# Layer 1's value products in 64x64 quadrants, with the second part moved behind the next half step's first scores

## The chip, the cores and the metric

The kernel runs on one core of a Trainium2 chip. A core has a matrix engine (TensorE, PE in the profile, with its weight loads shown apart as PEld), a vector engine (VectorE, DVE), a scalar engine (ScalarE, ACT), GpSimd (POOL) and a sync engine (SyncE, SP), which here issues nearly all DMA transfers. The metric is the device time of one execution in microseconds (us). Three runs of the kernel before took 4215.25 to 4218.63 us, with a median of 4215.89.

## What is computed

The input is a batch of 8 images with 512 channels of 32 x 32 pixels, so 1024 tokens each, in fp32. Two attention layers follow one another, each with a residual connection and a group normalization ahead of it. Layer 0 is ordinary attention with 8 heads of 64 channels. Layer 1, where the change lies, mixes the heads' scores before its softmax and normalizes the result over a whole head:

```python
attn = jnp.einsum('bhdq,bhdT->bhqT', q, k) * scale
attn = jnp.einsum('gh,bhqT->bgqT', w_head, attn)
attn = jax.nn.softmax(attn, axis=-1)
mean = jnp.mean(attn, axis=(-2, -1), keepdims=True)
var = jnp.var(attn, axis=(-2, -1), keepdims=True)
attn = (attn - mean) / jnp.sqrt(var + EPS)
attn = attn * in_gamma[None, :, None, None] + in_beta[None, :, None, None]
out = jnp.einsum('bhqT,bhdT->bhqd', attn, v)
```

After that come a projection with a bias and the residual.

## The kernel before

Layer 0 runs for all images first, layer 1 after it, image by image. The order of the instructions on every engine is the order in which the program writes them: nothing is rearranged by a scheduler[...]. An agenda (`ag`) holds pieces of work for fixed half steps.

In layer 1 an image has 4 blocks of 256 queries, and each block meets 4 blocks of 256 keys. Each of these 16 raw tiles is worked on in two half steps, so there are NX = 32 half steps `x`, and a few more in which the last ones drain. `half_step` interleaves three stages of different age:

- `scores(x, i)`, for i = 0 and 1: two heads each time, 8 matmuls in 64x64 quadrants, into one of three rotating PSUM tiles "m" of two banks. ACT or DVE copies the tile to `raw`. DVE does it for i = 0 in odd half steps, ACT for the rest. From half step 5 on, each part of the scores lets SP issue one piece of the next image's data or weights.
- `regroup`: eight DMA transfers of 256 KB (`re<-raw`) bring one raw tile into the order in which heads can be mixed, one region r each. One is issued after each part of a mix and each part of the value products, held by `behind` until the last matmul of that part is done.
- `mix(y, j)`, with y = x - 4: 32 matmuls of 64x64 with the head weights, region by region in the order `R_ORDER`, so the last 8 of its 64 records in the trace need the region that was sent last. ACT takes the exponential into `e` (two tiles rotate).
- With w = x - 5: `squares` on ACT, `sum_e` and `sum_e2` on DVE, and `values(w, 0)` and `values(w, 1)` on PE. Each part of the value products covers four heads, two in each column half, with all 128 keys as the contracted dimension; it adds to one of two accumulators `acc` of one PSUM bank each.

After every eighth value step the accumulators are copied out (`leave`), and `totals` sums the rows with 8 matmuls of 32 columns of weights (L1781). In fp32 a matmul shows as two records in the trace, each with a weight load before it, so 8 matmuls of scores are 16 matmul records, a mix part is 64, a value part is 8.

The instructions of one half step on PE stand in this order: scores part one, mix part one, value part one, scores part two, mix part two, value part two. On ACT: squares, scores copy (even half steps), squares, exponential, scores copy, exponential.

Of the kernel before, what the change touches and what calls it, by code (L numbers as in the profile page):

```python
# [18 lines left out]
P = 128  # L19
# [448 lines left out]
def tile_two_attention_layers(  # L468
# [19 lines left out]
    nc = tc.nc  # L488
    B, C, T = x_d.shape
    H = w_head.shape[0]  # L490
    D = C // H
    NCC = C // P
    NT = T // P
# [5 lines left out]
    Q8 = D // H  # L499
# [71 lines left out]
    NQB = 4  # L571
# [32 lines left out]
    class GroupStats:  # L604
# [3 lines left out]
        def __init__(self, pool, psum, mv, nm, keep=3):  # L608
            self.keep = keep
            self.pool, self.psum, self.mv, self.nm = pool, psum, mv, nm  # L610
            self.w = mv.shape[1]
# [85 lines left out]
    with ExitStack() as l0:  # L697
# [87 lines left out]
        n_t, xa_t, q_t, k_t, v_t = {}, {}, {}, {}, {}  # L785
# [415 lines left out]
        for b in range(B):  # L1201
            more = b + 1 < B
            ag = Agenda()
# [61 lines left out]
    with ExitStack() as l1:  # L1265
# [14 lines left out]
        NX = 2 * NQB * NKB  # L1280
        QLAG = NX // NQB
        R_ORDER = (0, 4, 1, 5, 2, 6, 3, 7)
        MLAG = 4

        def m_psum(nm):
            return ps_m.tile([P, 2, FB], F32, tag="m", name=nm)
# [4 lines left out]
        y_t, qo_t, k_t, v_t = ({0: t["1"]} for t in (n_t, q_t, k_t, v_t))  # L1291
        w_t = {}

        def behind(dma, ins):

            tc.add_manual_dep(
                dma.ins,
                ins.ins.name,
                mybir.DependencyInfo(
                    mybir.DependencyClass.Sync, mybir.DependencyReason.DATA  # L1300
                ),
                reason="one at a time",
            )
# [158 lines left out]
        def k_leave():  # L1462
            for fn in due:
                fn()
            due.clear()
# [173 lines left out]
        class Attention1:  # L1639
            def __init__(self, b):  # L1640
                self.b = b
                self.raw, self.re, self.e, self.e2 = {}, {}, {}, {}
                self.due, self.pieces = [], []

            def scores(self, x, i):

                b, t, hp = self.b, x // 2, x % 2 * 2 + i
                qb, kb = t // NKB, t % NKB
                nm = f"s1_{b}_{x}_{i}"
                ps = m_psum(nm)  # L1650
                pv = ps.rearrange("p m (j k) -> p m j k", j=2)
                for j in range(2):
                    for c in range(2):
                        for m in range(2):
                            r = slice(m * D, m * D + D)
                            last = nc.tensor.matmul(  # L1656
                                pv[c * D : c * D + D, m, j],
                                qo_t[b][r, 2 * qb + j, hp, ts(c, D)],
                                k_t[b][r, hp, ts(kb, KB)], start=True, stop=True,
                            )  # L1660
                if x > MLAG:
                    self.piece(last)
                if x % 2 and i == 1:
                    self.due = [(t, r) for r in R_ORDER]
                if x % 2 == 0 and i == 0:
                    self.raw[t] = rawpool.tile([P, H, 2, KB], F32, tag="raw", name=f"raw_{b}_{t}")
                dst = self.raw[t][:, 2 * hp : 2 * hp + 2]
                if i == (x == 0) and (x < MLAG or x % 2):
                    nc.vector.tensor_copy(dst, pv)  # L1669
                else:  # L1670
                    nc.scalar.copy(dst, pv)  # L1671

            def regroup(self, ins=None, n=1):

# [63 lines left out]
            def values(self, y, w):  # L1738

                b, t, kc = self.b, y // 2, y % 2  # L1740
                kc = t % NKB * 2 + kc
                if kc == 0 and w == 0:
                    self.acc = [
                        ps_a.tile([P, 2, QB], F32, tag=f"a{i}", name=f"a1_{b}_{y}_{i}")
                        for i in range(2)
                    ]
                e = self.by_head(self.e[y].rearrange("p j c -> p (j c)"))
                for g in range(4 * w, 4 * w + 4):
                    s, two = g // 2 % 2, g % 2
                    last = nc.tensor.matmul(  # L1750
                        self.acc[w][two * D : two * D + D, s].rearrange(
                            "p (c i) -> p c i", i=Q8
                        ),
                        v_t[b][:, kc, ts(g, D)], e[:, g],
                        start=(kc == 0 and s == 0), stop=(kc == NT - 1),
                        skip_group_check=True,
                    )
                self.regroup(last)

            def leave(self, qb):  # L1760
# [115 lines left out]

            def half_step(self, x, ag):
                y, w = x - MLAG, x - MLAG - 1
                if 0 <= w < NX:
                    self.squares(w, 0)  # L1880
                    self.sum_e(w, 0)
                if x < NX:
                    self.scores(x, 0)
                if 0 <= w < NX:
                    self.squares(w, 1)
                    self.sum_e(w, 1)
                if x < NX + MLAG:
                    k_leave()
                if 0 <= w < NX:
                    self.sum_e2(w, 0)  # L1890
                    self.sum_e2(w, 1)
                k_leave()
                if 0 <= y < NX:
                    self.mix(y, 0)
                if 0 <= w < NX:
                    self.values(w, 0)
                if x < NX:
                    self.scores(x, 1)
                if 0 <= y < NX:
                    self.mix(y, 1)  # L1900
                if x < MLAG or x >= NX:

                    self.regroup(n=NR if x != MLAG - 1 else 5)
                if x >= NX:
                    self.piece(n=len(self.pieces))
                ag.run(x - 0.5)
                if 0 <= w < NX:
                    self.values(w, 1)
                    self.e.pop(w)
                    if w % QLAG == QLAG - 1:  # L1910
                        qb = w // QLAG
                        self.leave(qb)
                        self.totals(qb)
                        if qb < NQB - 1:
                            ag.at(x + 2, lambda: self.reciprocals(qb, ag, x + 2))
                            ag.at(x + 6, lambda: self.divide(qb))
                ag.run(x)

        def load_wv_again(b):
# [7 lines left out]
        for b in range(B):  # L1927
            more = b + 1 < B
            a = Attention1(b)
            ag = Agenda()  # L1930
# [131 lines left out]
```

## Time and profile before

| What | Value |
|---|---|
| Median of three runs | 4215.89 us |
| Profiled execution, its span | 4215.8 us |
| PE busy | 4147.3 us (98%) |
| DVE busy | 2868.0 us (68%) |
| ACT busy | 2318.4 us (55%) |
| Layer 1's scores (L1656) | 552.0 us, 8192 records |
| Layer 1's mixes (L1704) | 596.5 us, 32768 records |
| Layer 1's value products (L1750) | 556.2 us, 4096 records |
| Granted PE clock | 0.999 |

The profiled execution is as long as the median of the runs. The span is that of the program's own instructions. Busy times of different lines may overlap. A line of the profile gives the source line, the engine, the operation, the tiles written and read, and the number of records. In brackets or after a second bar stands the idle time of the engine before the instruction and what ended it; "issue" means that the profile shows nothing that the engine waited for. A timeline or a chain has the start and the length in microseconds first. A matmul's end in the records is modelled, and records overlap, so a time from one start to the next is the surer measure.

Layer 1's half steps begin at about 1800 us. The second image's scores start at 2115.3 us and the third's at 2425.1.

### The profile page before, as it was taken

Reading aid. Unit: us, or ns where it says so; the run is one execution under the profiler, and the core shown is the slowest. Engines: PE = TensorE matmul, PEld = TensorE weight load, DVE = VectorE, ACT = ScalarE, POOL = GpSimd, SP = SyncE. Lnnn points to the kernel's source line nnn. Section 1 sums busy time; section 2 is a strip of 40 time slices with the busy share of each in tenths; the row PEclk is TensorE's granted clock in tenths of the full one; section 3 lists DMA queues with packets and bytes.
Section 4 is the critical chain, followed back from the end, with each engine's and each line's share of the span. In section 5 each row is a group of like instructions: output and inputs, shape, how many; then the busy total and the mean of one; then the engine's idle time right before and its main releaser. Section 6 shows DMA issues by size and latency. Waiting matters only on the chain.

```text
span 4215.8 us, 131422 instructions
## 1 busy us (share of the span) xinstructions
PE 4147.3 (98%) x58572; PEld 2216.2 (53%) x58572; DVE 2868.0 (68%) x3779; ACT 2318.4 (55%) x2735; POOL 60.3 (1%) x86
## 2 busy tenths in 40 slices
PE   8999999999999999999999999999999999999998
PEld 4353535353535353466466466466466466465565
DVE  5748484848484747568668668578578588587587
ACT  2717171727272625258268278278287287286386
POOL 0000000000000000000000000000000000000000
PEclk9999999999999999999999999999999999999999
DMA  4212121212121212167467377377386386485575
GB/s 132 97 65 94 59 101 50 82 45 84 48 84 48 84 48 84 62 156 196 131 170 188 121 189 189 108 201 190 104 206 177 112 208 159 129 209 145 148 180 138
DMA packets 257905, 529.35 MB, mean 126 GB/s; under 512 B 52336, under 2 KB 59888, under 8 KB 250672
## 3 DMA queue, kind: packets, MB, share of 16 engines
q1 hardware_dynamic: 254752, 520.15, 43.5%
q8 instruction: 461, 7.55, 0.8%
q0 software_dynamic: 2576, 0.69, 0.4%
q14 instruction: 116, 0.95, 0.1%
HBM read 204.50 MB, written 46.92 MB: 60 GB/s over the span
## 4 chain that ended last, share of the span: by engine, by line
PE 93%; DMA 2%; DVE 2%; ACT 1%; issue 1%; SPq 0%; DVEq 0%; ACTq 0%
PE a L1750 12%; PE m L1704 12%; PE s L1656 11%; PE s L1082 10%; PE a L1108 10%; PE pk_p L902 5%; PE pq_p L902 5%; PE pv_p L902 5%; PE pp_p L902 5%; PE pk L1400 4%; PE pq L1400 4%; PE pv L1475 4%; PE pp L1400 3%; PE t L1781 1%; DMA re<-raw 1%
## 5 line engine op out<-in xcount | busy, mean ns | idle before, releaser
L1704 PEld LDWEIGHTS m<-wmix,re 64*64 64x64 f32 x32768 | 583.6, 135 | 119.6 <-issue 53.5
L1087 ACT ACTIVATE e<-s 128x1024 f32<-128x1024 f32 x512 | 497.2, 1026 | 234.3 <-PE s L1082 233.8
L1704 PE MATMUL m<-wmix,re 64*64 64x64 f32 x32768 | 596.5, 219 | 21.1 <-issue 14.0
L1710 ACT ACTIVATE e<-m 128x1024 f32<-128x1024 f32 x512 | 525.2, 1026 | 141.9 <-PE m L1704 137.2
L1728 DVE TENSOR_TENSOR z<-z,e 128x1024 f32<-128x1024 f32 x448 | 538.0, 1219 | 68.8 <-ACT e L1710 68.7
L1732 DVE TENSOR_TENSOR z<-z,e 128x1024 f32<-128x1024 f32 x448 | 535.1, 1220 | 66.3 <-ACT e L1721 64.7
L1750 PE MATMUL a<-e,v 128*64 128x256 f32 x4096 | 556.2, 392 | 1.7 <-issue 1.0
L1656 PE MATMUL s<-k,q 64*64 64x256 f32 x8192 | 552.0, 388 | 5.0 <-DVE q L1512 2.7
L1095 DVE TENSOR_TENSOR zacc<-zacc,e 128x1024 f32<-128x1024 f32 x384 | 468.7, 1221 | 79.1 <-ACT e L1087 56.8
L1671 ACT COPY raw<-s 128x1024 f32<-128x1024 f32 x368 | 372.6, 1013 | 265.5 <-PE s L1656 226.5
L1082 PE MATMUL s<-q,k 64*64 64x512 f32 x4096 | 490.1, 593 | 2.3 <-ACT e L1087 2.3
L1108 PE MATMUL a<-e,v 64*64 64x512 f32 x4096 | 484.0, 589 | 0.0
L1721 ACT ACTIVATE e<-e 128x1024 f32<-128x1024 f32 x448 | 459.8, 1056 | 0.0
L1656 PEld LDWEIGHTS s<-k,q 64*64 64x64 f32 x8192 | 268.5, 132 | 267.8 <-issue 164.4
L1750 PEld LDWEIGHTS a<-e,v 128*64 128x64 f32 x4096 | 250.8, 136 | 122.5 <-issue 14.0
L1108 PEld LDWEIGHTS a<-e,v 64*64 64x64 f32 x4096 | 156.7, 133 | 282.8 <-issue 282.5
L1082 PEld LDWEIGHTS s<-q,k 64*64 64x64 f32 x4096 | 147.9, 133 | 275.2 <-issue 241.0
L1669 DVE COPY raw<-s 128x1024 f32<-128x1024 f32 x144 | 175.9, 1222 | 93.5 <-PE s L1656 89.7
L1093 DVE TENSOR_TENSOR zacc<-e,e 128x1024 f32<-128x1024 f32 x64 | 78.3, 1223 | 53.6 <-ACT e L1087 53.6
L1475 PE MATMUL pv<-wv,y 128*128 128x512 f32 x256 | 114.1, 599 | 0.5 <-DVE raw L1669 0.5
L1480 DVE COPY v<-pv 128x512 f32<-128x512 f32 x30 | 20.7, 690 | 136.0 <-ACT v L1479 136.0
L902 PE MATMUL pv_p<-left_v,tmp 128*128 128x256 f32 x512 | 113.1, 379 | 0.0
(316 smaller groups left out, 4162.7 us busy)
## 6 DMA issues: line engine op xcount, KB each, us to landing
re<-raw SPq DMA_DIRECT2D x1024, 256.0 KB
rzb<-zd SPq DMA_DIRECT2D x256, 128.0 KB
left_q<-left_q SPq DMA_DIRECT2D x17, 1792.0 KB
left_p<-left_p SPq DMA_DIRECT2D x17, 1792.0 KB
left_k<-left_k SPq DMA_DIRECT2D x10, 1792.0 KB
x<-in_x_dram SPq DMA_DIRECT2D x32, 512.0 KB
x<-x SPq DMA_DIRECT2D x64, 256.0 KB
left_v<-left_v SPq DMA_DIRECT2D x8, 1792.0 KB
```

The source lines that it names most:

```text
L902: nc.tensor.matmul(out, st, mv, start=start, stop=(k == 1), skip_group_check=True)
L1082: nc.tensor.matmul(ps[c * D : c * D + D, m], k[r, hp, k0 : k0 + D], q[r, hp, ts(f, FB)], start=True, stop=True,)
L1087: nc.scalar.activation(e[i], ps, AF.Exp, scale=S0 * S0)
L1095: nc.vector.tensor_add(zacc[g], zacc[g], e[i])
L1108: nc.tensor.matmul(acc[g][a][m * D : m * D + D], v[rows, kc, ts(2 * hp + m, D)], e[i][rows, m], start=(kc == 0), stop=(kc == NG - 1),)
L1400: nc.tensor.matmul(self.ps[m][:, i], w[:, left, k * HC + i * P : k * HC + i * P + P], right[:, k], start=(k == 0 and m != 2), stop=(k == 1 ...
L1656: last = nc.tensor.matmul(pv[c * D : c * D + D, m, j], qo_t[b][r, 2 * qb + j, hp, ts(c, D)], k_t[b][r, hp, ts(kb, KB)], start=True, stop=True,
L1704: last = nc.tensor.matmul(ps[c * D : c * D + D, a, ts(r, D)], self.re[t, r][rows, j, k0 : k0 + D], wmix[rows].rearrange("p g i -> p (g i)" ...
L1710: nc.scalar.activation(self.e[y][:, j], ps.rearrange("p a c -> p (a c)"), AF.Exp)
L1728: nc.vector.tensor_add(self.z[:, j], self.z[:, j], self.e[y][:, j])
L1732: nc.vector.tensor_add(self.z2[:, j], self.z2[:, j], self.e2[j])
L1750: last = nc.tensor.matmul(self.acc[w][two * D : two * D + D, s].rearrange("p (c i) -> p c i", i=Q8), v_t[b][:, kc, ts(g, D)], e[:, g], sta ...
```

## The change

The value products of the steps 0 to 26 are cut in quadrants: each matmul contracts 64 keys, and the two row halves work at the same time on different heads and in different accumulators. The second part of a step swaps the accumulators between the row halves, and the next step's first part goes on with that assignment. So a step has twice as many matmuls for its value products, 8 in each part (16 records). The last five steps (QF = 5) keep the old shape.

The second part is no longer issued at the end of its half step but in the next one, behind the first part of its scores, together with all that follows it there: the transfer of `regroup`, and, where a query block ends, `leave` and `totals`. Where the next value step begins a new query block, the second part comes ahead of those scores. The first matmul of each second part also waits until the most recent part two of the scores has been copied out of PSUM.

```diff
+        QF = 5
...
+                self.swap = self.late = None
...
                 if i == (x == 0) and (x < MLAG or x % 2):
-                    nc.vector.tensor_copy(dst, pv)
+                    out = nc.vector.tensor_copy(dst, pv)
                 else:
-                    nc.scalar.copy(dst, pv)
+                    out = nc.scalar.copy(dst, pv)
+                if i:
+                    self.swap = out
...
-                for g in range(4 * w, 4 * w + 4):
-                    s, two = g // 2 % 2, g % 2
-                    last = nc.tensor.matmul(
-                        self.acc[w][two * D : two * D + D, s].rearrange(
-                            "p (c i) -> p c i", i=Q8
-                        ),
-                        v_t[b][:, kc, ts(g, D)], e[:, g],
-                        start=(kc == 0 and s == 0), stop=(kc == NT - 1),
-                        skip_group_check=True,
-                    )
+                final = y >= NX - QF
+                for s in range(2):
+                    for n in range(2 if final else 4):
+                        if final:
+                            two, rows, half = n, slice(0, P), w
+                        else:
+                            two, a = n % 2, n // 2
+                            rows, half = slice(a * D, a * D + D), a ^ w ^ y % 2
+                        g = 4 * half + 2 * s + two
+                        last = nc.tensor.matmul(
+                            self.acc[half][two * D : two * D + D, s].rearrange(
+                                "p (c i) -> p c i", i=Q8
+                            ),
+                            v_t[b][rows, kc, ts(g, D)], e[rows, g],
+                            start=(kc == 0 and w == 0 and s == 0),
+                            stop=(kc == NT - 1 and (final or w == 1)),
+                            skip_group_check=True,
+                        )
+                        if w and self.swap is not None:
+                            behind(last, self.swap)
+                            self.swap = None
                 self.regroup(last)
...
             def half_step(self, x, ag):
                 y, w = x - MLAG, x - MLAG - 1
+
+                def finish():
+                    if self.late is not None:
+                        self.late()
+                        self.late = None
+
+                if w % QLAG == 0:
+                    finish()
                 if 0 <= w < NX:
                     self.squares(w, 0)
                     self.sum_e(w, 0)
                 if x < NX:
                     self.scores(x, 0)
+                finish()
...
                 if 0 <= w < NX:
-                    self.values(w, 1)
-                    self.e.pop(w)
-                    if w % QLAG == QLAG - 1:
-                        qb = w // QLAG
-                        self.leave(qb)
-                        self.totals(qb)
-                        if qb < NQB - 1:
-                            ag.at(x + 2, lambda: self.reciprocals(qb, ag, x + 2))
-                            ag.at(x + 6, lambda: self.divide(qb))
+
+                    def second():
+                        self.values(w, 1)
+                        self.e.pop(w)
+                        if w % QLAG == QLAG - 1:
+                            qb = w // QLAG
+                            self.leave(qb)
+                            self.totals(qb)
+                            if qb < NQB - 1:
+                                ag.at(x + 2, lambda: self.reciprocals(qb, ag, x + 2))
+                                ag.at(x + 6, lambda: self.divide(qb))
+
+                    if x + 1 < NX:
+                        self.late = second
+                    else:
+                        second()
                 ag.run(x)
```

## The prediction

> **What bounds the kernel now.** I read the page's busy shares first, then the chain that ended last, then TensorE's (PE's) timeline in single stretches.
>
> ```profile
> PE 4147.3 (98%) x58572; PEld 2216.2 (53%) x58572; DVE 2868.0 (68%) x3779; ACT 2318.4 (55%) x2735; POOL 60.3 (1%) x86
> q8 instruction: 461, 7.55, 0.8%
> ```
>
> PE carries the span. The last column of the first row matters later: 58572 matmul and 58572 weight-load records are 117144 PE instructions. The second row, of the DMA queues, is the traffic that brings instructions: 461 packets and 7.55 MB, so 16 KB or some 255 instructions a packet.
>
> The chain in order of time, at the third image's start (us, length, what):
>
> ```profile
> 2447.12 1.02 PE s L1656 x16
> 2448.15 0.93 PE m L1704 x64
> 2449.08 0.87 PE s L1656 x16
> 2449.95 0.96 PE m L1704 x64
> 2450.91 0.87 PE s L1656 x16
> 2451.77 0.93 PE m L1704 x64
> 2452.70 1.01 PE a L1750 x8
> 2453.72 1.02 PE s L1656 x16
> 2454.74 0.93 PE m L1704 x64
> 2455.67 1.01 PE a L1750 x8
> ```
>
> Scores (s) and mixes (m) are 64x64, value products (a) 128x64. Scores cost 0.87 behind a mix and 1.02 behind value products; these cost 1.01. A round of scores (four quadrants, 256 columns) and a round of value products (two column halves) start 0.216 us apart, so both have 0.86 of work (four rounds) and the rest, about 0.15 on each side, is the change of shape. An undisturbed half step is 2 x (1.02 + 0.93 + 1.01) = 5.92 us (5.94 from start to start).
>
> The half steps are not all undisturbed. From the start of half step 5 to that of 31 the first seven images take 165.2 us on average; less 3 x 1.87 for the row totals (L1781) that is 159.6 / 26 = 6.14 each. PE's timeline shows two kinds of stop, both inside a mix:
>
> ```profile
> 2200.00 0.99 PE L1704 MATMUL m<-wmix,re 64*64 64x64 f32 x56
> 2202.29 0.34 PE L1704 MATMUL m<-wmix,re 64*64 64x64 f32 x8 [1.30 <-DMA re<-raw]
> ```
>
> ```profile
> 2787.88 1.10 PE L1704 MATMUL m<-wmix,re 64*64 64x64 f32 x63
> 2789.55 0.27 PE L1704 MATMUL m<-wmix,re 64*64 64x64 f32 x1 [0.56 <-issue]
> ```
>
> The first waits for the eighth regrouped part of a raw tile (its last 8 matmuls). The second waits for nothing the profile shows. I counted PE instructions from one such "issue" stop to the next: 1024, 3071, 513, 1791, 1024, 1281, 2303 ..., multiples of 256 within two. They are the ends of fetched blocks. In the trace's packet times, 51 such stops of layer 1 have: the next fetch packet starts 1.50 us after the stop (1.06 to 2.4), ends 2.64 after it, and a block's first instruction runs 1.43 (spread 0.10) after its packet ended. So a block asked for when the one before begins is ready 4.07 us later. A half step holds 2 x (32 + 128 + 16) = 352 instructions, 1.375 blocks: 5.60 us of fetching beside 5.92 of work. It is hidden, but barely: these stops cost some 24 us, the re<-raw ones 8.5, in all of layer 1.
>
> [...]
>
> **The change, part by part.** Layer 0 already has value products in quadrants, row halves on different banks:
>
> ```profile
> 200.71 1.90 PE L1108 MATMUL a<-e,v 64*64 64x512 f32 x16
> 202.54 0.64 PE L1127 MATMUL z<-zacc,ones 128*32 128x256 f32 x8
> ```
>
> 16 records of 512 columns in 1.83 us: four at a time, 0.46 a round, where one 128x128 matmul of 512 columns takes 7.06 / 16 = 0.44 (L1475): next to no loss. So I price a 256-column round at 0.216.
>
> 1. Shape. For value steps 0 to 26 (half steps 5 to 31, 54 groups an image, 432 in all) each group goes from 8 records to 16, in four rounds of 0.216: 0.87. Both drains go. A half step of PE work becomes 2 x (0.87 + 0.93 + 0.87) = 5.34, 0.58 less; over 27 x 8 = 216 half steps that is 125 us, if nothing else takes its place. Groups 27 to 31 keep the old shape.
>
> 2. Instructions. 16 more matmuls and their loads per half step: 384 instead of 352, exactly 1.5 blocks. At 4.07 that is 6.10 us, 0.76 more than the new PE work. The cover that hid the fetch is gone: this takes the place of the drains.
>
> 3. Second part behind the next scores. The same PE instructions in another order; nothing is issued twice. Its re<-raw issue on SP's queue moves behind the next scores' piece transfer, so three issues now follow value part two, mix and value part one, 0.87 to 0.93 apart, where eight backlogged ones land about 1.05 apart (2124 to 2130 us). The eighth then lands some 0.3 later. Its landing takes 4.10 us on average from issue now (tiles 2 to 11, spread 0.61; 3.76 for tiles 12 to 14). At the new full speed the mix needs it 4.2 after issue; at the fetch's pace about 4.8. I allow 0.03 us a half step for it.
>
> 4. The new wait, on ScalarE's (ACT's) copy of the second scores. Queued behind it on PE: the mix and the next value part. That mix waited for the same copy, so only 0.87 us of slack goes. ACT has 11 instructions in two half steps, about 0.93 from start to start when back to back: 10.3 us, against 12.2. The copy is done before PE comes to it unless the eighth part is late by a further 0.6. Priced at nothing; without that cover ACT's chain makes a pair of half steps the landing time plus 6.9 us (0.2 to see the landing, four ACT instructions 3.9, then value part two, mix and value part one 2.7, and 0.1 to issue). DVE: 9 x 1.135 = 10.2 us a pair, also covered.
>
> 5. At steps 8, 16 and 24 the second part goes ahead of the first scores, with the accumulators' copies and row totals, as before.
>
> Sum for one image. Half steps 5 to 26 without the two that hold totals: 20 x (6.14 - 6.12) = 0.4 us. Half steps 27 to 31 without one: fewer transfers beside the fetch, which I estimate 0.2 us quicker, so 1.5 x 3.87 = 5.8 plus 0.05 against 6.1: 4 x 0.25 = 1.0. Three with totals: now 8.0; then 5.34 + 1.87 is more than 416 / 256 x 4.07 = 6.6, so PE sets it, with 0.2 for stops 7.4: 1.8. Together 3.2; times 8, 26 us. The profiled execution took 4215.8 us, as the median of the runs, 4215.89, so no correction: 4215.8 - 26 = 4190 us.
>
> The uncertain size is the 4.07. About 36 blocks an image, 288 in all, are paced by it, so 0.1 us is 29 us. It was measured where stops were rare[...]. From below: the shortest start, packet and delay seen (1.06, 0.88, 1.25) make 3.19, and then PE, ACT and landings pace instead. From above: the mean with one spread of its parts, 4.3. I take the mean.
>
> **Rivals.**
> - Fetch stays hidden, because blocks are asked for earlier than I read. Then ACT's chain behind the eighth landing paces: 4.4 + 6.9 = 11.3 us a pair, 5.65 a half step: 20 x 0.49 + 3 x 0.8 + 4 x 0.6 = 14.6 an image, 4099 us. For it: many blocks now pass in 3.55 us without a stop. Against: PE had run ahead there; after a stop the next packet is never sooner than 1.06.
> - Slower, by the fetch[...]. From 4.19 us a block the kernel is over 0.2% slower; at 4.22, 4233 us. For it: single fetches took up to 5.1, and the DMA share is 0.86 in such a stretch (2484 to 2490 us). Against: the pace, and so the traffic, is no higher than now.
> - Quadrants don't run four wide, as e is read with a stride: rounds of 0.43, a group of 1.73, 432 x (1.73 - 1.16) = 246 more, 4460. It decides from 0.29 a round. Against: now both column halves read that stride at full rate.
> - The drain is not the shape's: nothing is saved, the fetch paces, and half steps stay at 6.1 to 6.2: about 4220. Against: scores behind a mix at 0.87.
>
> **Numbers.** The fetch paces near 4.07: 0.52 (4150 to 4222). Fetch hidden: 0.13. Fetch over 4.19: 0.28. Quadrants narrow: 0.03. Drain stays: 0.04. Of the first, 0.11 lies within 0.2% (8.4 us, about what a measurement can tell from no change) and 0.41 below; of the last, 0.02 same and 0.02 slower. So faster 0.54, same 0.13, slower 0.33. The range for 8 in 10, 4125 to 4258, reaches from blocks at 3.85 to 4.3; the likeliest case's own is given above.
>
> **What would show it.** Right: value groups at 64x64 with 0.87 from start to start, scores behind them 0.87, no drains; "issue" stops at most blocks, some three in two half steps, as often in scores and value products as in mixes; half steps near 6.1; PE's busy share lower, with 58572 + 432 x 8 = 62028 records of each kind. Wrong: half steps of 5.6 with waits on ACT or re<-raw (fetch hidden), half steps over 6.3 (fetch slower), value groups over 1.2 us (quadrants narrow).

## The result

The changed kernel is slower. Its median is 4268.93 us (4266.87 to 4272.9), beside 4217.26 us for the kernel before in the same comparison: a ratio of 1.012, with a 95% interval of 1.0106 to 1.0135. The prediction was 4190 us and faster; the sign was wrong, the time missed by 79 us, and it lies above the predicted range (4125 to 4258).

These are the rows of the page of the changed kernel that answer to the first ones shown of before: engine busy times, the queue that brings instructions, and the groups of mixes and value products (busy, mean ns | idle before and what ended most of it).

```profile
PE 4075.1 (95%) x62028; PEld 2355.5 (55%) x62028; DVE 2870.2 (67%) x3779; ACT 2316.2 (54%) x2735; POOL 60.3 (1%) x86
q8 instruction: 488, 8.00, 0.8%
L1708 PE MATMUL m<-wmix,re 64*64 64x64 f32 x32768 | 656.6, 220 | 124.2 <-issue 105.5
L1761 PE MATMUL a<-e,v 64*64 64x256 f32 (+1 forms) x7552 | 577.9, 380 | 16.3 <-ACT raw L1673 9.9
```

PE is busy for 72 us less (4147.3 before), and idle for 124 us more (192.8 of 4267.9 instead of 68.5 of 4215.8). It has the 62028 records and the instruction queue the additional packets that were expected. The idle time lies mostly ahead of mixes.

PE's timeline at the third image shows the new half step (start, length, what; in brackets the idle time just before and what ended it):

```profile
2519.88 1.13 PE L1708 MATMUL m<-wmix,re 64*64 64x64 f32 x64
2520.81 1.06 PE L1658 MATMUL s<-k,q 64*64 64x256 f32 x16
2521.68 1.06 PE L1761 MATMUL a<-e,v 64*64 64x256 f32 x16
2522.54 0.90 PE L1708 MATMUL m<-wmix,re 64*64 64x64 f32 x48
2523.91 0.35 PE L1708 MATMUL m<-wmix,re 64*64 64x64 f32 x8 [0.47 <-issue]
2525.13 0.34 PE L1708 MATMUL m<-wmix,re 64*64 64x64 f32 x8 [0.88 <-DMA re<-raw]
2525.30 1.05 PE L1761 MATMUL a<-e,v 64*64 64x256 f32 x16
2526.16 1.04 PE L1658 MATMUL s<-k,q 64*64 64x256 f32 x16
2527.03 1.11 PE L1708 MATMUL m<-wmix,re 64*64 64x64 f32 x64
```

From start to start a mix takes 0.93 (2519.88 to 2520.81), scores 0.87 (2520.81 to 2521.68, and behind value products 2526.16 to 2527.03) and value products 0.86 (2521.68 to 2522.54 and 2525.30 to 2526.16). In the records of the value products at 2521.68 four records start within 0.04 us and the next four 0.216 later, where the old shape has two records to such a round (2455.60 before): the row halves do work at the same time. The 0.15 us on each side of the value products, which the prediction puts down to the change of shape and calls drains, is gone. In its place the mix at 2522.54 is stopped twice, 0.47 us by nothing that the profile shows and 0.88 by the last regrouped part. So PE is also held back where the profile shows no semaphore. PE's waits over the whole execution (us in total, times, longest):

```profile
PE m L1708 <- issue: 105.5, 130, 2.1
PE m L1708 <- DMA re<-raw: 16.5, 22, 2.4
PE a L1761 <- ACT raw L1673: 9.9, 22, 1.5
PE a L1761 <- issue: 5.6, 11, 1.1
```

The kernel before has, in the same view:

```profile
PE m L1704 <- issue: 14.0, 28, 1.1
PE m L1704 <- DMA re<-raw: 5.7, 10, 1.3
```

This view counts a stop only where the engine's records leave a gap. Counted from start to start, over what a group takes undisturbed, layer 1's stops are: issue 142 us (176 stops) where before had 24 (50), re<-raw 20 (8.5), ACT's copy 11 (0.6), ACT's exponential 6 (0.2). Nearly all issue stops of layer 1 stand at multiples of 256 instructions from one another, before and after, as the prediction read them. Of those in the view of gaps all 31 distances before and all 148 after are such multiples within one, if PE's semaphore instructions are counted too. Every packet of the instruction queue has 16384 bytes, and there are 124056 / 488 = 254 matmul and load instructions to a packet; a packet takes 1.10 us on average, and the first instruction after a stop runs 1.43 us after a packet ended, in both traces. That PE's instructions are fetched in blocks of 256 is read from these numbers.

For all runs below I use one measure beside the time: the mean time from one image's first scores of layer 1 to the next image's, over seven images. It is 307.8 us before and 314.5 after; 8 x 6.7 = 54 us is the whole difference, so it lies in layer 1.

### The profile page after: what moved, and what is told of

It reads as the page before. It is cut to its first block, busy times and chain, and to the rows that moved or that the text cites. A ratio compares the mean times of both kernels' runs of the same rounds, so it can differ in the third digit from the quotient of the medians.

```text
span 4267.9 us, 138296 instructions
## 1 busy us (share of the span) xinstructions
PE 4075.1 (95%) x62028; PEld 2355.5 (55%) x62028; DVE 2870.2 (67%) x3779; ACT 2316.2 (54%) x2735; POOL 60.3 (1%) x86
## 4 chain that ended last, share of the span: by engine, by line
PE 84%; DMA 5%; ACT 4%; issue 4%; DVE 3%; SPq 0%; ACTq 0%; DVEq 0%
PE s L1082 10%; PE a L1108 10%; PE m L1708 9%; PE a L1761 9%; PE s L1658 8%; PE pk_p L902 5%; PE pq_p L902 5%; PE pv_p L902 5%; PE pp_p L902 5%; PE pk L1401 4%; PE pq L1401 4%; PE pv L1476 4%; DMA re<-raw 4%; PE pp L1401 3%; PE t L1796 1%
## 5 line engine op out<-in xcount | busy, mean ns | idle before, releaser
L1708 PE MATMUL m<-wmix,re 64*64 64x64 f32 x32768 | 656.6, 220 | 124.2 <-issue 105.5
L1708 PEld LDWEIGHTS m<-wmix,re 64*64 64x64 f32 x32768 | 638.4, 135 | 208.5 <-issue 155.1
L1761 PE MATMUL a<-e,v 64*64 64x256 f32 (+1 forms) x7552 | 577.9, 380 | 16.3 <-ACT raw L1673 9.9
L1658 PE MATMUL s<-k,q 64*64 64x256 f32 x8192 | 570.4, 380 | 10.8 <-issue 3.2
L1658 PEld LDWEIGHTS s<-k,q 64*64 64x64 f32 x8192 | 350.2, 133 | 117.2 <-issue 47.8
L1761 PEld LDWEIGHTS a<-e,v 64*64 64x64 f32 (+1 forms) x7552 | 336.5, 134 | 98.4 <-issue 25.2
L902 PE MATMUL pq_p<-tmp,left_q 128*128 128x512 f32 x256 | 112.5, 593 | 0.0
```

The source lines that it names most:

```text
L902: nc.tensor.matmul(out, st, mv, start=start, stop=(k == 1), skip_group_check=True)
L1658: last = nc.tensor.matmul(pv[c * D : c * D + D, m, j], qo_t[b][r, 2 * qb + j, hp, ts(c, D)], k_t[b][r, hp, ts(kb, KB)], start=True, stop=True,
L1708: last = nc.tensor.matmul(ps[c * D : c * D + D, a, ts(r, D)], self.re[t, r][rows, j, k0 : k0 + D], wmix[rows].rearrange("p g i -> p (g i)" ...
L1761: last = nc.tensor.matmul(self.acc[half][two * D : two * D + D, s].rearrange("p (c i) -> p c i", i=Q8), v_t[b][rows, kc, ts(g, D)], e[rows ...
```

## The experiments

The theory to begin with: the fetch of PE's instructions in blocks of 256 paces the changed kernel. The rival: its order does, by the later landing of the eighth regroup transfer and by the new wait for ACT's copy.

**The order alone (order_alone).**

```diff
-        QF = 5
+        QF = NX
...
-                            start=(kc == 0 and w == 0 and s == 0),
+                            start=(kc == 0 and s == 0 and (final or w == 0)),
```

> The changed kernel with every value product in the old 128x64 shape (QF = NX): the moved second part, the later regroup transfer and the new wait stay, the instructions of a half step go back from 384 to 352. If the fetch of instructions (4.12 us for 256 of them) sets the changed kernel's pace, this one is within some 15 us of the kernel before: 4205 to 4230 us, with some 25 us of stops named issue in layer 1 instead of 142. If the new order loses the time (the wait for the scores' copy, the eighth regroup part that lands later), it stays at 4250 us or more, with long waits on re<-raw and on ACT's copy.

4220.19 us, ratio 1.0017 (1.001 to 1.0024), 308.7 us an image. Its waits on PE:

```profile
PE a L1761 <- ACT raw L1673: 12.9, 33, 1.0
PE m L1708 <- issue: 10.3, 21, 1.4
PE m L1708 <- DMA re<-raw: 5.5, 12, 1.1
```

This is what the expectation gave for the fetch. With 352 instructions in a half step the moved second part and its wait cost 7 to 8 us. The eighth transfer lands 4.14 us after its issue here, as before (4.10); in the changed kernel it is 4.54. So the order in itself explains little of the 52 us.

**Fewer PE instructions (after_half_mix, before_half_mix).** In both kernels:

```diff
-                for r in R_ORDER:
+                for n, r in enumerate(R_ORDER[1::2]):
...
-                                ps[c * D : c * D + D, a, ts(r, D)],
+                                ps[c * D : c * D + D, a, ts(n, P)].rearrange(
+                                    "p (u x) -> p u x", u=2
+                                ),
...
-                                wmix[rows].rearrange("p g i -> p (g i)"),
+                                wmix[rows].rearrange("p g i -> p (g i)")
+                                .unsqueeze(1).to_broadcast([D, 2, D]),
```

> The changed kernel with half as many instructions in its mixes: only every second region is mixed, each with 128 columns (the head weights twice) instead of 64, so PE's work in a mix stays about 0.93 us, but a half step issues 256 PE instructions instead of 384, which is one fetched block of 4.12 us beside 5.34 us of work. The output is not the reference's, since half of the mixing is left out and the other half is written twice. If the fetch sets the changed kernel's pace, nearly all of the 142 us of issue stops go and the time falls to 4050 to 4120 us (half steps of 5.4 to 5.65). If order and waits set it, it stays above 4200 us, with the waits on re<-raw, on ACT's copy and on the exponential grown in the place of the stops.

> The kernel before with the same cut of its mixes: 224 PE instructions in a half step instead of 352, the same columns. Again half of the mixing is left out. Both theories say that the fetch costs this kernel little: its 24 us of issue stops in layer 1 go and the time is 4185 to 4200 us. Its distance to the changed kernel with the same cut is what the shape and the order are worth without the fetch: some 100 us in the changed kernel's favour by the fetch theory, none or the other sign by the order theory. If the time falls by far more than 24 us, the shorter list of weight loads makes a mix itself quicker, which the mix groups then show.

One run each, so without a spread, beside 4212.3 us for the kernel before: 4174.31 us with the changed kernel's order and shape, 4153.19 us with the kernel before's. The first page row of each, and the waits of the changed one:

```profile
PE 4019.9 (96%) x45644; PEld 2168.3 (52%) x45644; DVE 2861.1 (69%) x3779; ACT 2306.0 (55%) x2735; POOL 60.3 (1%) x86
PE m L1708 <- DMA re<-raw: 71.7, 73, 2.2
PE a L1764 <- ACT raw L1673: 27.8, 32, 1.7
```

```profile
PE 4097.3 (99%) x42188; PEld 2119.4 (51%) x42188; DVE 2864.5 (69%) x3779; ACT 2307.8 (56%) x2735; POOL 60.3 (1%) x86
```

None of the expected times was met. In the changed kernel with fewer instructions every issue stop is gone and 95 us with them, of which the shorter mixes account for up to 22 (below), so the fetch did pace it. But it does not come down to 4050 to 4120: the landings take over. Half steps alternate 5.29 and 6.6 us, 11.9 a pair, and ACT's timeline shows where the longer one waits:

```profile
2530.64 1.01 ACT L1673 COPY raw<-s 128x1024 f32<-128x1024 f32 x1 [1.28 <-DMA re<-raw]
```

The copy of new scores waits here until the eighth transfer has read the old raw tile (there are two): 1.28 us, and 55.3 us in 44 such waits over the execution. This is the prediction's ACT chain, landing plus 6.9 us: the landing is 4.70 us in this run, which makes 11.6. The kernel before with the same cut has steady half steps of 5.82 us, where uncut it has 5.92 of work and takes 6.14. The mixes are thus some 0.05 us shorter each, 0.10 x 216 = 22 us of the 59 that this run gained, where I had expected 12 to 27 in all. The other 37 went with the issue stops, which show 24; the waits on re<-raw did not go (9.1 us here in the view of gaps, 5.7 before).

The distance between the two runs has the sign that the order theory gave: the changed kernel is 21 us slower, not some 100 faster. So with the fetch out of the way the landings alone take the whole gain, and neither theory is enough by itself.

**The second part in its old place (in_place).**

```diff
-                    if x + 1 < NX:
-                        self.late = second
-                    else:
-                        second()
+                    second()
```

> The changed kernel with the second part of the value products back at the end of its half step, behind mix two: quadrants, 384 instructions and the wait for ACT's copy stay. By the fetch theory the fetch still sets the pace, and the wait, which now has only a mix of 0.93 us between the copied scores and the waiting value part, adds up to the 0.42 us that it cost where that stands so in the changed kernel: between 4265 us (all of it beside the fetch) and 4360 us (216 half steps x 0.42 on top). By the order theory the regroup transfer goes out earlier again and the time falls below 4255 us.

4267.4 us, ratio 1.0131 (1.0114 to 1.0148): inside what the fetch theory gave, and the time of the changed kernel, from quite other waits.

```profile
PE m L1708 <- issue: 62.8, 93, 1.6
PE a L1761 <- ACT raw L1673: 61.4, 165, 1.5
PE m L1708 <- DMA re<-raw: 3.1, 7, 0.8
```

The wait for the copy is six times as long (61.4 us beside 9.9), the stops named issue in mixes are shorter by nearly as much (62.8 beside 105.5), and the time is the same. A pace set by the fetch would look like this, if a wait inside a block is paid out of the stop at its end. But the equal time is also luck: the blocks are ready sooner here (3.96 us beside 4.12), and more is lost inside them (62 us beside 29, by the last table of this section). So the run shows that putting the second part back does not help; it does not show that the wait is free.

**384 instructions in the kernel before (before_split_1).**

```diff
+                            cuts = (0, D // 2, D) if r == R_ORDER[0] else (0, D)
+                            for lo, hi in zip(cuts, cuts[1:]):
...
-                                ps[c * D : c * D + D, a, ts(r, D)],
+                                    ps[c * D : c * D + D, a, r * D + lo : r * D + hi],
...
-                                wmix[rows].rearrange("p g i -> p (g i)"),
+                                    wmix[rows].rearrange("p g i -> p (g i)")[:, lo:hi],
```

> The kernel before, unchanged but for the mixes of one of the eight regions: each of their matmuls is cut in two of 32 columns. The same sums in the same order, the same PE columns (5.92 us of work in a half step), but 384 PE instructions in a half step instead of 352, the number of the changed kernel. If 384 instructions cannot be fetched within a half step, 1.5 x 4.12 = 6.18 us is the least that a half step takes, against 6.14 now, plus what blocks of uneven work lose: 15 to 50 us slower, 4227 to 4262 us, with stops named issue at over 100 us in layer 1 instead of 24. If the changed kernel's loss is the order and the landings alone, this one stays within 8 us of the kernel before.

4296.72 us, ratio 1.0203 (1.0186 to 1.022), more than either theory gave, and for a reason that makes the run useless for the question. This run, and below it the same mix in the kernel before:

```profile
2522.80 1.29 PE L1706 MATMUL m<-wmix,re 64*64 64x32 f32 x72
2524.02 1.08 PE L1752 MATMUL a<-e,v 128*64 128x256 f32 x8
```

```profile
2454.56 1.11 PE L1704 MATMUL m<-wmix,re 64*64 64x64 f32 x64
2455.60 1.08 PE L1750 MATMUL a<-e,v 128*64 128x256 f32 x8
```

From its start to that of the value products behind it a mix takes 1.22 us instead of 1.04: cutting columns was not free here. With 6.3 us of work in a half step the issue stops are only 31 us.

**No late landings, and neither (after_four_regions, after_neither).** The first leaves out half of the transfers; the second adds the mixes of 128 columns, over `R_ORDER[:4]`.

```diff
                 for t, r in self.due[:n]:
...
+                    if r in R_ORDER[4:] and (self.b or t > 1):
+                        continue
                     dma = nc.sync.dma_start(out=self.re[t, r], in_=self.raw[t][r::NR])
```

> The changed kernel in which only the first four of the eight regions of a raw tile are transferred (from the third tile of the first image on), so that no mix waits for a late landing and ACT's copy finds its raw buffer free early; the other four regions are mixed from old data, so that part of the scores is not used. PE's instructions are all there, 384 in a half step. If the fetch alone sets the pace, blocks of 4.12 us (less, if half the transfers make the fetch quicker; I estimate down to 3.9) give 5.85 to 6.3 a half step: 4170 to 4245 us, with issue stops of 100 us and more. If the landings alone set the pace, half steps fall to PE's 5.34 and the time to 4040 to 4110 us, with the issue stops gone.

> Both cuts in the changed kernel: the mixes use the first four regions alone, with 128 columns each (256 PE instructions in a half step), and only these four are transferred. Half of the mixing is left out, and the other half written twice. If fetch and landings are all that keeps the quadrants from their gain, every half step is near the 5.29 us that an undisturbed one takes with such a mix: 4035 to 4080 us. If something else limits (ACT with 10.3 us in two half steps, DVE with 10.2, the wait for the scores' copy), it stays above 4100 us, and the waits name it.

The first run took 13968.93 us, because its stale scores set off a general path that the program holds behind the fast one, and that runs where the softmax's sums leave their range. Only the fast part can be read: 303.5 us an image, 11.0 less than the changed kernel; 8 x 11.0 = 88 us less would be some 4181 us, inside what the fetch theory gave; it is an estimate from the images and not a measured time. PE's waits in that part (1830 to 4190 us):

```profile
PE m L1710 <- issue: 57.6, 90, 2.3
PE a L1763 <- ACT raw L1673: 12.9, 21, 1.6
```

No wait on re<-raw is left, and stops remain (89 us from start to start, where 100 and more were expected): the fetch still sets the pace, but a quicker one (a block is ready after 3.91 us instead of 4.12, in the tables below). The second run took 4064.68 us (288.5 us an image), as expected, with both limits gone:

```profile
PE a L1766 <- ACT raw L1673: 24.0, 32, 1.7
PE s L1658 <- ACT e L1719: 5.4, 7, 0.8
```

Its undisturbed half steps are 5.20 to 5.29 us against 5.82 in the kernel before with mixes of the same shape: 0.53 to 0.62, where the prediction had 0.58 for the change of shape. The gain of the shape is real. Two limits stand in front of it. Each of these two runs is a single one, and the kernel before was not run with both cuts.

**The transfers (after_two_first, before_two_first).** To take the landing waits away without touching PE's work, the first two of the eight go out together, so that the eighth leaves one place earlier:

```diff
-                self.regroup(last)
+                self.regroup(last, 2 if len(self.due) == NR else 1)
```

> The changed kernel, but of the eight regroup transfers of a raw tile the first two go out together behind the first free mix part, so that each later one, the eighth too, goes out one place earlier (0.87 us and more before the mix that needs it). All PE work and all 384 instructions stay. If I take each block of 256 PE instructions of the changed kernel as the larger of its own work and 4.12 us, an image's half steps 5 to 31 come to 164.4 us, against 169.8 measured; if the 5.4 us left are late landings and what hangs on them, up to 8 x 5.4 = 43 us go: 4225 to 4250 us. If everything is the fetch, it stays at 4255 to 4275 us, with the issue stops grown by what the waits lose.

> The same edit in the kernel before. Its waits on re<-raw are 8.5 us in all of layer 1, and the block account (the larger of a block's work and 4.07 us) already gives 165.8 us for half steps 5 to 31, against 165.1 measured. So at most these 8.5 us are to be had: 4200 to 4212 us, the same as before or little less. Above 4220 us, two transfers at once would slow the fetch itself.

4280.85 us (1.017, 1.015 to 1.0191) and 4255.2 us (1.0095, 1.0078 to 1.0111). PE's waits in the first and in the second:

```profile
PE m L1708 <- issue: 146.6, 145, 2.1
PE s L1658 <- issue: 11.8, 14, 1.4
```

```profile
PE m L1704 <- issue: 48.9, 55, 2.0
PE a L1750 <- issue: 5.8, 6, 1.3
```

In both the waits on re<-raw are gone altogether, and both became slower, by longer issue stops; both times lie above what was expected. The transfers act on the fetch: with two together the mean fetch of a block goes from 3.82 to 4.04 us in the kernel before (last table), which costs it some 40 us. For that reason the time of the first run doesn't tell whether the landing was a second loss beside the fetch; the last table of this section does.

**A shape that costs no instructions (adjacent, adjacent_two_first, adjacent_three_first).** The value products stay 128x64, but part two of one step and part one of the next follow one another behind the first scores (two_first and three_first add the edit above, with 2 or 3).

```diff
+                if w % QLAG == 0:
+                    finish()
...
                     self.scores(x, 0)
+                finish()
+                if 0 <= w < NX and x < NX:
+                    self.values(w, 0)
...
-                if 0 <= w < NX:
+                if 0 <= w < NX and x >= NX:
                     self.values(w, 0)
```

`finish` and the late second part are those of the changed kernel.

> The kernel before with its 128x64 value products and 352 PE instructions, but with the second part of one step and the first part of the next put next to each other behind the first scores of a half step. The shape changes twice in a half step instead of four times: 0.3 us less, so 5.62 us of PE work, beside 1.375 x 4.12 = 5.67 us of fetching on average. The eighth regroup transfer goes out one group earlier against the mix that needs it. By the fetch theory half steps come to 5.75 to 5.95 instead of 6.14: 4160 to 4185 us, faster than both kernels. If a moved second part loses by itself (order and landings), it is 4210 us or more.

> The order with both value parts next to each other (128x64, 352 instructions), and the first two regroup transfers sent together. With the adjacent parts the waits on the exponential and the copies, behind ACT's wait for re<-raw, took 25 us or more, and the issue stops 59 us. By the block account this order should take 5.98 us a half step where the kernel before takes 6.20, 0.22 x 216 = 47 us less; it was 21 us slower. If the late landings ate that, sending the eighth transfer earlier brings 4175 to 4205 us, faster than the kernel before. If the fetch is slower here for its own reasons, it stays at 4215 to 4235 us.

> As before, with the first three regroup transfers sent together, which puts the eighth one more place ahead. If landings are still late with two, another 5 to 15 us go; if three transfers at once slow the fetch or the pieces behind them, it is slower than with two by 5 us or more.

4231.82 us (1.0052, 1.0035 to 1.0069), 4264.62 us (1.0124, 1.0108 to 1.0139) and 4292.3 us (1.0192, 1.0176 to 1.0207): all slower than the kernel before, the bunched ones most, where the fetch theory had 4160 to 4185 for the first and 4175 to 4205 was hoped for from the second. From start to start the issue stops are 59, 111 and 126 us, the waits on ACT's exponential 22, 7 and 6. This order puts PE's instructions together less evenly: a block that starts with a mix holds 128 + 32 + 96 instructions and 2.5 us of work, less than the 3.93 us that a fetch takes here on average. That takes back much of the saving, but the 5.98 us a half step of the second expectation was too low: redone from its parts (5.62 of work, 4.12 a block) the block account gives 6.1, which would still be faster than the 6.20 of the kernel before. The rest was lost inside the blocks (last table), where the eighth transfer lands 4.51 us after its issue (4.10 before).

**Evenly spaced transfers (before_even, after_even, adjacent_even).** Since two at once had come with longer issue stops, I spaced them, none later than it was (in after_even a piece of the next image also moves). In the kernel before (the others likewise, as their expectations say):

```diff
+                    if r == R_ORDER[3]:
+                        self.regroup(last)
                 nc.scalar.activation(self.e[y][:, j], ps.rearrange("p a c -> p (a c)"), AF.Exp)
-                self.regroup(last)
```

> The kernel before with each regroup transfer that followed a mix part let go in the middle of that part: the four of a half step then go out about 1.48 us apart instead of 0.99 and 1.98, and none later than now. Two at once cost the kernel before 42 us, with issue stops of 68 instead of 24 us. If it is the bunching that makes the fetch of instructions slow, even spacing makes it quicker: issue stops below 20 us, no waits on re<-raw, 4190 to 4208 us. If two at once cost for another reason, this one is at 4208 to 4225 us.

> The changed kernel with the four transfers of a half step evenly spaced, about 1.33 us: behind the first scores, in the middle of both mixes and behind value part one; the piece of the next image that stood behind the first scores follows value part two. The changed order had put three of them 0.87 to 0.93 apart. If that bunching is what made the fetch and the landings slow, the block time falls from 4.12 towards 3.9, the re<-raw waits go, and the time falls to 4200 to 4245 us. If the number of instructions alone sets it, it stays at 4255 to 4275 us.

> The order with both value parts next to each other, 352 instructions, and the transfers spaced evenly, 1.25 to 1.4 us (behind the first scores, in the middle of value part one, behind mix one, in the middle of mix two), each as early as now or earlier; a piece follows value part two. Bunched by two and three it took 4265 and 4292 us, as first written 4232. If bunching slows the fetch, issue stops fall from 59 to 35 us or less and the time to 4165 to 4205 us, faster than both kernels. Otherwise 4220 to 4240 us.

4222.03 us (1.0009, 1.0 to 1.0017), 4294.1 us (1.0176, 1.016 to 1.0192) and 4249.34 us (1.0073, 1.0059 to 1.0086). The idea fell: even spacing helps nowhere and costs the changed kernel 25 us. The time from a stop until the next block can run is 4.27 us in after_even and 4.12 in the changed kernel; in the kernel before it went from 4.07 to 4.23. No version that does all the work is faster than the kernel before.

**What a block takes.** In each trace I took all stretches from one issue stop to another that are a whole number of 256 instructions long, between half steps 5 and 31. "Ready" is the mean time from a stop until the following block can run, from the packets (as the prediction worked it out). "Pace" is what a block in these stretches took.

| Kernel | blocks | work, us | ready, us | pace, us |
|---|---|---|---|---|
| changed kernel | 281 | 3.65 | 4.12 | 4.32 |
| in_place | 269 | 3.65 | 3.96 | 4.31 |
| after_two_first | 280 | 3.64 | 4.20 | 4.39 |
| after_even | 289 | 3.64 | 4.27 | 4.46 |
| after_four_regions | 259 | 3.64 | 3.91 | 4.07 |

In these runs the pace follows the time of the fetch, 0.16 to 0.20 us above it; in_place, whose blocks also hold 70 us of waits for the copy, lies 0.35 above. The changed order has no worse a pace than the old one. 85 of the changed kernel's blocks have a stop at both ends and no whole block between: 4.26 us, spread 0.42.

"Ready" counts only blocks that follow a stop. The packets allow the same for every block: each can run 1.43 us after its own packet ended (in the traces of the kernel before, the changed one, in_place and after_even no block began sooner than 1.20 after). "Own fetch" is the mean time from the start of a block until the next can run. The three sums are over all blocks that lie wholly between half steps 5 and 31 of an image, in us: their work, priced with the sizes above; the larger of work and own fetch, block by block; and what they took.

| Kernel | own fetch, us | work | work or fetch | measured |
|---|---|---|---|---|
| kernel before | 3.82 | 1239 | 1271 | 1285 |
| changed kernel | 4.08 | 1122 | 1301 | 1330 |
| order_alone | 3.74 | 1235 | 1260 | 1289 |
| in_place | 3.92 | 1126 | 1270 | 1332 |
| before_two_first | 4.04 | 1239 | 1314 | 1328 |
| after_two_first | 4.17 | 1122 | 1330 | 1346 |
| before_even | 3.85 | 1239 | 1277 | 1295 |
| after_even | 4.24 | 1122 | 1343 | 1369 |
| adjacent | 3.93 | 1181 | 1255 | 1286 |
| after_four_regions | 3.77 | 1122 | 1232 | 1252 |

What the last column has over the one before it was lost inside the blocks. In the changed kernel the 162 of 307 blocks that end in a stop last 4.36 us on average, beside an own fetch of 4.35: there the fetch accounts for all of it. A tenth of a microsecond in the 1.43 would move some 10 us in the kernel before and 20 in the changed one between these two columns. (Where the second part is moved, this stretch holds one value part less an image, some 7 us in all.) In the changed kernel 117 us less work become 30 us more once each block waits for its own packet, and 29 are lost inside instead of 14. Putting the second part back saves 31 there and loses 33 more inside. Sending two transfers first saves 13 inside and costs 29 of fetch; in the kernel before it costs 43 of fetch, the whole of its loss. Adjacent parts save 58 of work, of which the fetch leaves 16, and lose 17 inside.

## Why the prediction was wrong

**Shape (step 1): right.** Value groups and the scores behind them take 0.87, and where neither fetch nor landings limit (after_neither), a half step loses 0.53 to 0.62 us (0.58 predicted).

**Instructions (step 2): right in kind, too small in size, and this is the step that failed.** 62028 records and a block that is ready 4.12 us after the last one began (4.07 predicted) came as said. Stops came at over half of the blocks (162 of 307) and not at nearly all, in value products and scores too, but mostly in mixes (130 of 149 in the view of gaps). The mistake was to take that mean as the pace, 1.5 x 4.07 = 6.10. The pace is 4.32. The first reason is that blocks hold unequal work: a half step's 384 instructions have 256 in mixes with 1.86 us of work, 128 in the rest with 3.48. A block of one and a half mixes and two other groups has 3.13 us, one with four other groups and one mix up to 4.41. A mean lets the long ones make up for the short ones; in this account they don't. If each block takes the larger of its own work and 4.12, half steps 5 to 31 of an image come to 164.4 us where the mean gave 161.7; measured are 169.8. The same account gives 165.8 for the kernel before (165.1 measured) and 165.3 for the order alone (164.7), and 158.2 with 3.91 for the four regions (159.8). So unevenness is 2.7 of the 8.1 us between mean and measurement. Of the other 5.4 some 3.7 were lost inside the blocks (29 us over 8 images), which leaves 1.7 to single fetches that are longer or shorter than the mean. The account with a mean fetch would thus have seen the changed kernel level with the one before (164.4 against 165.8), not 52 us slower.

Where the 79 us are: the 18 half steps of an image clear of totals take 6.40 instead of 6.12, 18 x 0.28 x 8 = 40 us (6.40 is 1.5 x 4.27). The half step with totals and the next take 14.50 together instead of 7.4 + 6.12, 3 x 0.98 x 8 = 24 us. The other 15 are in the last half steps and what follows them.

**Landing (step 3): wrong in size, a second and smaller loss.** The eighth transfer lands 0.44 us later (0.3 predicted), and the waits are 20 us, not the 6 allowed (the sum's 6.12 should have been 6.13 with them). With those waits gone (after_two_first) 13 us less are lost inside the blocks, but the same edit makes the fetch slower by more.

**The new wait (step 4): small, but not nothing.** It was priced at nothing because the copy would be done before PE came to it; it stops PE 27 times, 11 us. How much of that the stops at the blocks' ends would have taken anyway is not shown. Where it is 70 us (in_place), 62 us are lost inside the blocks instead of 29. No run has the quadrants without this wait or without the exchange of the accumulators, so what either is needed for is not shown.

**The totals (step 5): wrong.** "As before" it isn't: the half step with totals was priced as bound by PE alone, and the pair around it takes 14.5 us, more than the 13.9 before.

**The rivals.** What happened is the second one, slower by the fetch: it put the turn at 4.19 us a block, and the pace of 4.32 lies beyond, though the mean readiness of 4.12 does not. The transfers have a part in it: with half of them a block is ready after 3.91 us and the pace is 4.07, and two sent together make the mean fetch longer (4.08 to 4.17, and 3.82 to 4.04 in the kernel before), but spacing them does not help (4.24). The 0.2 us by which the sum took the fetch to be quicker beside fewer transfers was an estimate of mine; the 3.91 beside 4.12 is of that size. The first, fetch hidden, is what after_half_mix shows: ACT's chain behind the landing at 11.9 us a pair, where the prediction had 11.3 with a shorter landing; even that run is only 38 us below the kernel before. Narrow quadrants and a drain that stays were rightly given little: a round takes 0.216 us, and the 0.15 us is gone.

I also misread the kernel before. Its half steps were 0.22 us over their work, which I took for scattered stops and compared with a mean fetch of 5.60. With fewer instructions it runs at its work (half steps of 5.82 us in before_half_mix), and with its own it loses 32 us to the fetch (1271 against 1239). To this kernel, which already waited for its instructions, the change added 32 in each half step.

## What to carry to other kernels

Where TensorE runs many short matmuls, count instructions beside columns. Look in the trace for stops named issue that are whole multiples of one number apart (256 here, with a mean fetch of 3.74 to 4.24 us a block in the last table). If they are there, take, block by block, the larger of its work and its fetch time, not the mean over a loop: here the mean gave 161.7 us for an image's half steps 5 to 31, the account by blocks 164.4, and 169.8 were measured. Where a trace has the packets, take each block's own; 14 to 62 us were lost inside the blocks on top of that in these runs. A saving of PE work that adds instructions has to be set against the fetch: here 117 us less work became 30 us more. And if a wait is removed and the time stays, look at what took its place before moving on to the next wait.

## What the runs showed of the hardware that was not expected

- Cutting 4 of the 32 matmuls of a mix into halves of 32 columns makes the mix 0.18 us longer (1.22 instead of 1.04), with the same columns in all. I have no explanation.
- Two 256 KB transfers let go together, instead of one, cost the kernel before about 0.95% (4255.2 us) though no wait on them is left; it is the instruction stops that grow, from 24 to 68 us, and the mean fetch of a block, from 3.82 to 4.04.
- In the changed kernel an even spacing of the same transfers makes the mean fetch of a block longer (4.08 to 4.24 us) than the uneven one, which has 0.87 to 2.07 us between two transfers. In the kernel before it hardly moves (3.82 to 3.85). No run shows why.
